# A sparse graph network of two layers: four edits to the attention vectors, the gathers and the column products

## The chip, the cores and the metric

The kernel runs on one core of a Trainium2 chip. The metric is device time in microseconds (us), the median of several runs. An execution recorded by the hardware profiler gives the traces shown here; it has a time of its own, which is stated beside them. TensorE is called PE, VectorE DVE, ScalarE ACT, GpSimd POOL and SyncE SP in the lines of the profile.

## The reference

A graph of 3327 nodes has one dense 0/1 adjacency matrix with ones on its diagonal, about nine ones in a row. Two layers work on 512 features per node, in fp32. Cut to what matters:

```python
def layer0(X, A, W, b, a_self, a_neigh):            # 4 heads of 128
    feats = einsum('nf,hfo->hno', X, W)
    logits = leaky_relu(e_s[:, :, None] + e_n[:, None, :], 0.2) + NEG_INF * (1 - A)
    out = softmax(logits) @ feats + b               # per head
    return relu(out)
x = layernorm(x + layer0(x, adj, ...))

def layer1(x, adj, W_sa, a_sa, W_g, b_g, Wa, ba, Wb, bb):
    gate_a = sigmoid(concat([adj @ x, x]) @ Wa.T + ba)      # gate_b alike
    h = x @ W_sa
    s_left, s_right = h @ a_sa[:512], h @ a_sa[512:]
    e = where(adj, exp(-leaky_relu(s_left + s_right.T, 0.01)), 0)
    x_a = (e / (sum(e) + 1e-5)) @ h
    x_b = adj @ (x @ W_g) + b_g
    return sigmoid(gate_a * x_a + gate_b * x_b)
x = layernorm(x + layer1(x, adj, ...))
```

Since only about nine entries of a row are not zero, the kernel turns each row of the matrix into a list of neighbours and gathers their rows. `s_left` and `s_right` are products of x with two vectors, `W_sa @ a_sa[:512]` and `W_sa @ a_sa[512:]`; these are "W_sa's vectors".

## The kernel before

The 3327 nodes are padded to 3328 and cut into 26 tiles of 128 nodes. The order of instructions on each engine is the order in which the program writes them; a tile framework adds the semaphores.

**Ahead of layer 0.** The node axis is cut into seven chunks of up to 512. For each chunk the kernel computes feature rows (`feature_sums`, L385, `feature_rows`), which go to a table in HBM (`table0`), and reads the chunk's columns of the matrix through 11 buffers with the tag "at" (L228, issued by SP, in order). `make_codes` (L430) packs 16 matrix rows into one number by a matmul with powers of two, `turn_codes` (L455) transposes the codes, `top_codes` takes the largest ones per node on VectorE (L73, L76), and `decode`, `pick`, `name` make neighbour lists of them. W_sa is loaded into two of the same "at" buffers (L244), between the loads of chunks 4 and 5. `scores_vectors` makes the vectors of it: for each of four blocks of 128 rows it transposes the block on PE (L362), copies it on ScalarE (L364), and multiplies it by `a_sa` (L366); the sums go into columns 0 and 3 of `v1`. The tail of the program's first part is `make_codes(4)`, `turn_codes(4)`, `top_codes(4)`, `scores_vectors()`, `make_codes(5)`, `turn_codes(5)`, `climb(0)`. Chunks 4 to 6 hold the second group of tiles; the rest of their lists is made inside layer 0, in its steps 0 to 7 (`lists`).

**Groups and stairs.** Nodes are sorted by degree within two groups of 12 and 14 tiles, so that each tile has a fixed number of neighbours (`CAPS`). The few nodes of very high degree sit in the first tile of each group; their surplus neighbours are spread over the 128 partitions of one extra row, the "stair". `climb` (L661 to L671) makes the list for that extra gather out of the sorted lists by one matmul.

**Layer 0** goes through the tiles in the order `order0`: 11, 10, 0, 1, 2, ... "Place" below is the index in that order. Every row is gathered by an indirect DMA of 128 rows of 520 numbers (L769), issued by POOL; a tile of the second group reads its own two rows by one more (L763), a stair is L778. Before the change the buffers are seven of six rows each, `GB = 7`, `U = 6`; a tile's rows are cut into equal pieces of at most six, one buffer each, and `AHEAD = 3` tiles are asked for in advance:

```python
        n = (c + more + U - 1) // U
        w = (c + more + n - 1) // n
```

Step i of the loop writes, in this order: the gathers of the tile three places on; the publishing of finished tiles (`publish`, with a scatter L147 for the second group); `columns2` of the tile two places back; `attend` of tile i; the relu and residual sum y of the tile before (L1034), its transposes (`columns1`, L940), its statistics; `columns3` of two back (L951); the lists; and the weights of the next tile (`weigh_a` L871 to L890 with the exponential L884, `weigh_b` L895 to L899). `attend` scales each gathered row by its weight, two of three rows on VectorE (L916), the third on ScalarE (L914), and sums them in PSUM by matmuls with the identity (L923). `columns2` copies the transposed tile from PSUM by ScalarE (L944) and multiplies it with the eight columns of `v1` (L947), which gives the scores that layer 1 needs.

**Layer 1** gathers the finished rows from `table1` through the same buffers (L769). Each tile has a weighted sum on VectorE (L1161, with L1163 for sums of two), a plain sum on PE (L1182), two transposes (L1192) and two products with W_sa and W_g (L1201). `weights_a` handles the gathered columns piece by piece: an addition (L1096), a reduction (L1105) and, from the second piece on, one more addition (L1116).

Of the kernel before, what the change touches and what calls it, by code (L numbers as in the profile page):

```python
# [14 lines left out]
P = 128  # L15
# [9 lines left out]
S = 24  # L25
# [6 lines left out]
U = 6  # L32
GB = 7
# [22 lines left out]
def row_bcast(src, n, offset=0):  # L56

    return bass.AP(tensor=src.tensor, offset=src.offset + offset, ap=[[0, P], [1, n]])
# [22 lines left out]
def sparse_pass(  # L81
# [160 lines left out]
    for k in range(0, KT, 2):  # L242
        wsa0 += [p0.tile([P, 2, CH], F32, tag="at", name=f"wsa0_{k}", bufs=AT)]
        nc.sync.dma_start(wsa0[-1], W_sa[k * P : (k + 2) * P, :].rearrange("(k p) o -> p k o", p=P))  # L244
    for i in range(5, len(chunks)):
        load_adj(i, 0, 3)
# [93 lines left out]
    with nc.allow_non_contiguous_dma(reason="four vectors of 512, onto partitions"):  # L340
        for i, w in enumerate((Wa, Wb)):
            for s in range(2):
                src = w[0:1, s * F : (s + 1) * F].rearrange("o (k p) -> p (o k)", p=P)
                nc.gpsimd.dma_start(v1[:, :, 3 * s + 1 + i], src)
        asa = p0.tile([P, KT, 2], F32, name="asa")
        for s in range(2):
            src = a_sa[0:1, s * F : (s + 1) * F].rearrange("o (k p) -> p (o k)", p=P)
            nc.gpsimd.dma_start(asa[:, :, s], src)
# [7 lines left out]
    def scores_vectors():  # L356

        sums = psl.tile([P, CH], F32, tag="pc1", name="asa_sums")[:, : 2 * KT].rearrange("p (k s) -> p k s", s=2)
        for k in range(KT):
            pt = psl.tile([P, CH], F32, tag="pc0", name=f"wsa_t{k}").rearrange("p (o w) -> p o w", o=KT)  # L360
            for o in range(KT):
                nc.tensor.transpose(pt[:, o, :], wsa0[k // 2][:, k % 2, o * P : (o + 1) * P], ident)  # L362
            turned_ = p0.tile([P, KT, P], F32, tag="v", name=f"wsaT{k}", bufs=2)
            nc.scalar.copy(turned_, pt)  # L364
            for o in range(KT):
                nc.tensor.matmul(sums[:, k, :], turned_[:, o, :], asa[:, o, :], start=(o == 0), stop=(o == KT - 1))  # L366
        nc.vector.tensor_copy(v1[:, :, 0], sums[:, :, 1])
        nc.vector.tensor_copy(v1[:, :, 3], sums[:, :, 0])
        nc.vector.tensor_add(v1[:, :, 4:6], v1[:, :, 4:6], v1[:, :, 1:3])
        nc.vector.tensor_add(v1[:, :, 6], v1[:, :, 0], v1[:, :, 3])  # L370
# [349 lines left out]
    make_codes(4)  # L720
    turn_codes(4)
# [4 lines left out]
    climb(0, p0, psl.tile([P, CH], F32, tag="pc0", name="climb0")[:, : B + H])  # L726
# [19 lines left out]
    def gather(table, j):  # L746


        g, i = place(j)
        ahead = 0 if table is table1 else 1 + g  # L750
        c = CAPS[j] + ahead
        more = j in T0
        n = (c + more + U - 1) // U
        w = (c + more + n - 1) // n
        got = []
        for q0 in range(0, c + more, w):
            m = min(w, c - q0)
            buf = gp.tile([P, U, ROW], F32, tag="g", name=f"g_{nc.next_id()}", bufs=GB)
            for q in range(q0, q0 + m):
                s = q - ahead + 1  # L760
                if ahead == 2 and q < 2:
                    if q == 0:
                        nc.gpsimd.indirect_dma_start(  # L763
                            out=buf[:, 0:2, :].rearrange("p t w -> p (t w)"), out_offset=None,
                            in_=own1.rearrange("n t w -> n (t w)"),
                            in_offset=bass.IndirectOffsetOnAxis(ap=srt[g][:, i, S + 1 : S + 2], axis=0),
                        )
                    continue
                nc.gpsimd.indirect_dma_start(  # L769
                    out=buf[:, q - q0, :], out_offset=None, in_=table[:, :],  # L770
                    in_offset=bass.IndirectOffsetOnAxis(ap=srt[g][:, i, s : s + 1], axis=0),
                )
            o = 1 if ahead == 2 and q0 == 0 else 0
            if m > o:
                got.append((q0 + o - ahead + 1, m - o, buf, o))
        if more:
            stair[j] = buf[:, m, :]
            nc.gpsimd.indirect_dma_start(  # L778
                out=stair[j], out_offset=None, in_=table[:, :],
                in_offset=bass.IndirectOffsetOnAxis(ap=ids2[g][:, 0:1], axis=0),  # L780
            )
        return got

    stair = {}
# [78 lines left out]
    got, ws, accs, ws2 = {}, {}, {}, {}  # L863

    def weigh_a(j):
# [20 lines left out]
        for s0, n, buf, o in got[j]:  # L886
            a = max(s0, 1)
            nc.scalar.copy(srt[g][:, i, a : s0 + n], buf[:, o + a - s0 : o + n, F + H])
# [12 lines left out]
    def attend(j, lean):  # L901
# [6 lines left out]
        for s0, n, buf, o in got[j]:  # L908
            for s in range(s0, s0 + n):
                k = 2 if s % 3 == 0 and s + 1 < s0 + n else 1  # L910
                gv = buf[:, o + s - s0 : o + s - s0 + k, 0:F].rearrange("p t (h o) -> p t h o", h=H)
                if s % 3 == 2:
                    for h in range(H):
                        nc.scalar.activation(gv[:, 0, h, :], gv[:, 0, h, :], AF.Copy, scale=w[:, s, h : h + 1])  # L914
                elif s % 3 == 0 or s == s0:
                    nc.vector.tensor_tensor(  # L916
                        gv, gv, w[:, s : s + k, :].rearrange("p t (h o) -> p t h o", o=1).to_broadcast([P, k, H, FO]),
                        ALU.mult,
                    )
                row = buf[:, o + s - s0, 0:F]  # L920
                if lean and s == 0:
                    nc.vector.tensor_add(row, row, bias0)
                nc.tensor.matmul(  # L923
                    acc, ident, row, start=(lean and s == 0), stop=(s == CAPS[j] and j not in T0)
                )
        if j in T0:
# [14 lines left out]

    def columns2(j):
        xt1 = m0.tile([P, KT, P], F32, tag="xt1", name=f"xt1_{j}")
        nc.scalar.copy(xt1, turned[j])  # L944
# [21 lines left out]
    AHEAD = 3  # L966
    for j in order0[:4]:
        own_x(j)
    for i in range(AHEAD):
        got[order0[i]] = gather(table0, order0[i])  # L970
# [41 lines left out]
    for i in range(NT + 3):  # L1012
# [7 lines left out]
        if i + AHEAD < NT:  # L1020
            j = order0[i + AHEAD]
            got[j] = gather(table0, j)
# [3 lines left out]
        if 2 <= i < NT + 2:  # L1026
            columns2(order0[i - 2])
        if i < NT:
            attend(order0[i], i >= 3)
        if 0 < i <= NT:  # L1030
# [3 lines left out]
            nc.vector.scalar_tensor_tensor(y, accs[j], 0.0, xj, ALU.max, ALU.add)  # L1034
            columns1(j)
# [170 lines left out]
    for i in range(3):  # L1206
        got[at_(i)] = gather(table1, at_(i))
# [5 lines left out]
    for i in range(NT + 3):  # L1213
        j, j1, jp, jpp = at_(i), at_(i + 1), at_(i - 1), at_(i - 2)
        if at_(i + 3) is not None:
            got[at_(i + 3)] = gather(table1, at_(i + 3))
# [494 lines left out]
```

## Time and profile before

| | us |
|---|---|
| median of 3 runs | 998.16 |
| lowest and highest | 991.17, 1000.08 |
| the profiled execution | 1102.09 |
| its span, first to last instruction | 1100.0 |

The profiled execution's granted PE clock is 0.856 of full speed in the mean. Over its span PE is busy 845.0 us (77%), VectorE 723.8 (66%), POOL 611.7 (56%), ScalarE 281.9 (26%).

| stage of the profiled execution | from, us | to, us |
|---|---|---|
| feature rows, codes, lists of the first group | 0 | 152 |
| chunk 5's codes, W_sa's vectors, first gathers | 152 | 205 |
| layer 0, places 0 to 8 with the lists of chunks 4 to 6 | 205 | 410 |
| layer 0, places 9 to 25 | 410 | 655 |
| layer 1, start | 655 | 720 |
| layer 1 | 720 | 1100 |

How to read it: a group's line has its line in the kernel, engine and operation, what it writes and reads, shapes and count; then its busy time and the mean of one in ns; then the idle time of its engine just before it, with what ended most of that. "Issue" is waiting for nothing that the profile shows; "remote" is a wait that ended by a semaphore for which no record of the profile stands. A fp32 matmul has two records, and a matmul's end is modelled, so its mean can be longer than the distance to the next one. Times are from the start of the span.

### The profile page before, as it was taken

Reading aid. Unit: us, or ns where it says so; the run is one execution under the profiler, and the core shown is the slowest. Engines: PE = TensorE matmul, PEld = TensorE weight load, DVE = VectorE, ACT = ScalarE, POOL = GpSimd, SP = SyncE. Lnnn points to the kernel's source line nnn. Section 1 sums busy time; section 2 is a strip of 40 time slices with the busy share of each in tenths; the row PEclk is TensorE's granted clock in tenths of the full one; section 3 lists DMA queues with packets and bytes.
Section 4 is the critical chain, followed back from the end, with each engine's and each line's share of the span. In section 5 each row is a group of like instructions: output and inputs, shape, how many; then the busy total and the mean of one; then the engine's idle time right before and its main releaser. Section 6 shows DMA issues by size and latency. Waiting matters only on the chain.

```text
span 1100.0 us, 10256 instructions
## 1 busy us (share of the span) xinstructions
PE 845.0 (77%) x2596; PEld 450.0 (41%) x2596; DVE 723.8 (66%) x2179; ACT 281.9 (26%) x824; POOL 611.7 (56%) x663
## 2 busy tenths in 40 slices
PE   6999761755785877668897685399797978997994
PEld 5777641322433333334443341144343434443442
DVE  3367740563895676556764574379797997997893
ACT  1122110220412132323434231032233213232322
POOL 6011646555474227467777627737777776777502
PEclk9999965668787879699888886699899998998998
DMA  9899888857966227487667616735666664666401
GB/s 320 351 372 409 313 325 305 258 156 230 317 171 180 68 83 218 141 299 205 187 195 207 197 50 185 203 108 155 196 172 187 183 193 147 188 189 176 123 10 60
DMA packets 72850, 220.89 MB, mean 201 GB/s; under 512 B 11472, under 2 KB 16544, under 8 KB 72016
## 3 DMA queue, kind: packets, MB, share of 16 engines
q0 software_dynamic: 44592, 146.73, 45.1%
q1 hardware_dynamic: 23200, 62.32, 15.2%
q10 hardware_dynamic: 4992, 11.12, 2.7%
q8 instruction: 23, 0.38, 0.1%
q14 instruction: 43, 0.35, 0.1%
HBM read 199.26 MB, written 28.32 MB: 207 GB/s over the span
## 4 chain that ended last, share of the span: by engine, by line
PE 36%; DVE 20%; issue 15%; POOL 9%; DMA 8%; another core or an unknown queue 8%; ACT 3%; DVEq 0%; ACTq 0%; POOLq 0%; SPq 0%
PE acc L923 15%; POOL g L769 8%; DVE sw L1161 7%; PE pf L385 7%; PE po L1201 5%; DMA g<-table,srt 4%; PE acc L1182 4%; DMA at<-in_adjB 3%; DVE g L1163 2%; PE pcol L947 2%; DVE g L916 1%; DMA xc<-in_xB 1%; PE pc L430 1%; ACT g L914 1%
## 5 line engine op out<-in xcount | busy, mean ns | idle before, releaser
L769 POOL DMA_INDIRECT g<-table,srt x464 | 489.0, 1054 | 265.8 <-issue 130.3
L923 PE MATMUL acc<-g,ident 128*128 128x512 f32 x504 | 265.9, 690 | 9.0 <-issue 5.6
L1161 DVE SCALAR_TENSOR_TENSOR sw<-g,e,sw 128x512 f32<-128x512 f32 x226 | 169.4, 750 | 12.8 <-issue 4.5
L923 PEld LDWEIGHTS acc<-g,ident 128*128 128x128 f32 x504 | 110.6, 225 | 147.9 <-issue 132.0
L1182 PE MATMUL acc<-g,ident 128*128 128x512 f32 x262 | 123.4, 606 | 13.1 <-DMA g<-table,srt 9.7
L1201 PE MATMUL po<-wsa,sT 128*128 128x512 f32 x208 | 99.8, 624 | 24.9 <-issue 16.2
L385 PE MATMUL pf<-w,xc 128*128 128x260 f32 (+1 forms) x416 | 102.7, 410 | 15.6 <-DMA xc<-in_xB 10.6
L916 DVE TENSOR_TENSOR g<-g,w 128x1024 f32<-128x1024 f32 (+1 forms) x102 | 105.1, 1073 | 1.1 <-DVE w L897 0.5
L385 PEld LDWEIGHTS pf<-w,xc 128*128 128x128 f32 x416 | 84.7, 206 | 31.4 <-issue 10.5
L947 PE MATMUL pcol<-v,xt 128*128 128x8 f32 x208 | 37.0, 305 | 78.5 <-ACT xt L944 39.1
L1201 PE MATMUL po<-wg,sT 128*128 128x512 f32 x208 | 93.7, 593 | 0.0
L914 ACT ACTIVATE g<-g,w 128x128 f32<-128x128 f32 x304 | 92.1, 393 | 0.9 <-issue 0.9
L1182 PEld LDWEIGHTS acc<-g,ident 128*128 128x128 f32 x262 | 50.2, 194 | 80.3 <-issue 52.0
L1201 PEld LDWEIGHTS po<-wsa,sT 128*128 128x128 f32 x208 | 41.2, 201 | 80.6 <-issue 69.3
L947 PEld LDWEIGHTS pcol<-v,xt 128*128 128x128 f32 x208 | 34.7, 252 | 85.1 <-ACT xt L944 43.4
L1163 DVE TENSOR_TENSOR g<-g 128x512 f32<-128x512 f32 x95 | 65.7, 692 | 3.3
L147 POOL DMA_INDIRECT out<-za,srt x26 | 29.0, 1117 | 58.6 <-ACT za L1246 52.5
L1194 ACT COPY sT<-pt 128x512 f32<-128x512 f32 x52 | 29.0, 588 | 120.6 <-remote 51.1
L1201 PEld LDWEIGHTS po<-wg,sT 128*128 128x128 f32 x208 | 39.4, 190 | 48.8 <-issue 48.3
L884 ACT ACTIVATE w<-w 128x40 f32<-128x40 f32 (+10 forms) x26 | 6.2, 238 | 192.9 <-DVE w L883 102.2
L73 DVE MAX8 ent<-pv 128x8 f32<-128x224 f32 x26 | 10.0, 386 | 51.9 <-PE pv L455 51.9
L401 ACT COPY row<-pf 128x512 f32<-128x512 f32 x26 | 15.3, 587 | 104.2 <-PE pf L385 66.6
(279 smaller groups left out, 948.8 us busy)
## 6 DMA issues: line engine op xcount, KB each, us to landing
at<-in_adjB SPq DMA_DIRECT2D x78, 512.0 KB
g<-table,srt POOLq DMA_INDIRECT x464
table<-row ACTq DMA_DIRECT2D x26, 260.0 KB
own<-in_xo SPq DMA_DIRECT2D x1, 3640.0 KB
own<-table SPq DMA_DIRECT2D x1, 3640.0 KB
at<-in_adjL SPq DMA_DIRECT2D x13, 256.0 KB
table<-x1a SPq DMA_DIRECT2D x12, 260.0 KB
xc<-in_xB ACTq DMA_DIRECT2D x3, 1024.0 KB
```

What stands on the lines that cost most here:

```text
L147: put = nc.gpsimd.indirect_dma_start(out=dst, out_offset=bass.IndirectOffsetOnAxis(ap=rows, axis=0), in_=src, in_offset=None, bounds_check ...
L385: nc.tensor.matmul(pf[:, hh, :w], xc[:, k, o : o + P], w0[:, k, hh, :w], start=(k == 0), stop=(k == KT - 1))
L769: nc.gpsimd.indirect_dma_start(out=buf[:, q - q0, :], out_offset=None, in_=table[:, :], in_offset=bass.IndirectOffsetOnAxis(ap=srt[g][:, i ...
L914: nc.scalar.activation(gv[:, 0, h, :], gv[:, 0, h, :], AF.Copy, scale=w[:, s, h : h + 1])
L916: nc.vector.tensor_tensor(gv, gv, w[:, s : s + k, :].rearrange("p t (h o) -> p t h o", o=1).to_broadcast([P, k, H, FO]), ALU.mult,)
L923: nc.tensor.matmul(acc, ident, row, start=(lean and s == 0), stop=(s == CAPS[j] and j not in T0))
L947: nc.tensor.matmul(pcol, xt1[:, k, :], v1[:, k, :], start=(k == 0), stop=(k == KT - 1))
L1161: nc.vector.scalar_tensor_tensor(sw, g[:, i, 0:F], e[:, s : s + 1], sw, ALU.mult, ALU.add)
L1163: nc.vector.tensor_add(g[:, i, 0:F], g[:, i - 1, 0:F], g[:, i, 0:F])
L1182: nc.tensor.matmul(plain[j], to, row, start=(not sums_of_two and i == 0), stop=(sums_of_two and i == len(rows) - 1),)
L1194: nc.scalar.copy(sT, pt)
L1201: nc.tensor.matmul(proj[j], sT[:, k, :], wt[:, k, :], start=(half + k == 0), stop=(half + k == KT))
```

## The change

- `scores_vectors` makes W_sa's vectors on VectorE: for each half of `a_sa` and each of four blocks of W_sa one product with a sum (`tensor_tensor_reduce`) straight into a column of `v1`. `a_sa` comes as two rows spread over all partitions, into a third "at" buffer, behind W_sa in SP's queue. The products are written into the pool `pj`, which is given back before the ring's memory is taken.
- `climb(0)` moves ahead of `turn_codes(4)`.
- The buffers of the gathers become one tile of 42 rows, `ring`. `plan` lays out all tiles of a layer in it one after another; a tile is cut only where the ring ends. `gather` issues, in order, whatever fits into 42 rows past the last tile that is given back by `free`. In layer 0 `gather` and `free` now stand behind y of the tile before, in layer 1 at the head of the step.
- `columns2` is split: ScalarE's copy (`columns2a`) stays ahead of `attend`, the eight matmuls are issued inside it, behind the rows 0 to 2 of the sum.

```diff
+    asa_rows = p0.tile([P, 2, CH], F32, tag="at", name="asa_rows", bufs=AT)
+    for s in range(2):
+        nc.sync.dma_start(asa_rows[:, s, :], row_bcast(a_sa, F, s * F))
...
     def scores_vectors():
-        sums = psl.tile([P, CH], F32, tag="pc1", name="asa_sums")[:, : 2 * KT].rearrange("p (k s) -> p k s", s=2)
-        for k in range(KT):
-            pt = psl.tile([P, CH], F32, tag="pc0", name=f"wsa_t{k}").rearrange("p (o w) -> p o w", o=KT)
-            for o in range(KT):
-                nc.tensor.transpose(pt[:, o, :], wsa0[k // 2][:, k % 2, o * P : (o + 1) * P], ident)
-            turned_ = p0.tile([P, KT, P], F32, tag="v", name=f"wsaT{k}", bufs=2)
-            nc.scalar.copy(turned_, pt)
-            for o in range(KT):
-                nc.tensor.matmul(sums[:, k, :], turned_[:, o, :], asa[:, o, :], start=(o == 0), stop=(o == KT - 1))
-        nc.vector.tensor_copy(v1[:, :, 0], sums[:, :, 1])
-        nc.vector.tensor_copy(v1[:, :, 3], sums[:, :, 0])
+        for s in range(2):
+            for k in range(KT):
+                prod = pj.tile([P, ROW], F32, tag="row", name=f"sprod{s}_{k}", bufs=4)[:, :F]
+                nc.vector.tensor_tensor_reduce(
+                    prod, wsa0[k // 2][:, k % 2, :], asa_rows[:, s, :], 1.0, 0.0, ALU.mult, ALU.add,
+                    v1[:, k, 3 - 3 * s : 4 - 3 * s],
+                )
...
     make_codes(4)
+    climb(0, p0, psl.tile([P, CH], F32, tag="pc0", name="climb0")[:, : B + H])
     turn_codes(4)
     top_codes(4)
     scores_vectors()
     make_codes(5)
     turn_codes(5)
-    climb(0, p0, psl.tile([P, CH], F32, tag="pc0", name="climb0")[:, : B + H])
...
+    ring = gp.tile([P, RING, ROW], F32, name="ring")
...
+        while s <= CAPS[j]:
+            n = 2 if own_x_too and s == 0 else 1
+            if planned[0] % RING + n > RING:
+                planned[0] += 1
+            p = planned[0] % RING
+            m = min(CAPS[j] + 1 - s + n - 1, RING - p)
+            buf = ring[:, p : p + m, :]
+            got[j].append((s, m - (n - 1), buf, n - 1))
...
+    def gather():
+        while waiting and waiting[0][0] - freed[0] <= RING:
+            indirect(*waiting.pop(0)[1:])
+
+    def free(j):
+        freed[0] = ends_at[j]
...
-        if 2 <= i < NT + 2:
-            columns2(order0[i - 2])
+        third = order0[i - 2] if 2 <= i < NT + 2 else None
+        if third is not None:
+            columns2a(third)
         if i < NT:
-            attend(order0[i], i >= 3)
+            attend(order0[i], i >= 3, lambda: third is None or columns2(third))
+        elif third is not None:
+            columns2(third)
...
             nc.vector.scalar_tensor_tensor(y, accs[j], 0.0, xj, ALU.max, ALU.add)
+            free(j)
+            gather()
             columns1(j)
```

In layer 1 the loop calls `free(jp)` for the tile before and `gather()` at the head of its step, in place of asking for the tile three places on.

## The prediction, made before the changed kernel ran

> **What bounds the kernel now.** I read first the busy time by stage (columns: stretch, length, busy time and instructions of PE, PE's weight loads, VectorE, ScalarE, POOL; then the granted PE clock, the share of the DMA engines and GB/s).
>
> ```profile
> 152.00:205.00 53.00, 21.23 (x100) 14.77 (x98) 11.69 (x46) 5.97 (x13) 29.16 (x31) 0.50 0.92 331
> 205.00:410.00 205.00, 144.27 (x371) 69.89 (x372) 137.47 (x459) 49.44 (x169) 99.95 (x99) 0.78 0.58 177
> 410.00:655.00 245.00, 191.36 (x535) 97.84 (x533) 148.37 (x426) 85.22 (x267) 156.28 (x144) 0.86 0.61 188
> 720.00:1100.00 380.00, 332.75 (x897) 156.67 (x895) 316.87 (x766) 105.20 (x241) 229.96 (x211) 0.95 0.51 148
> ```
>
> Layer 1 (from 720) is full: PE is busy 88%, VectorE 83%. Layer 0 (205 to 655) is not: no engine is busy over 78%. So layer 0 waits for something, and the waits (us in total, times, longest) say for what. POOL between 340 and 480, then VectorE between 410 and 625:
>
> ```profile
> POOL g L769 <- PE acc L923: 40.6, 5, 18.5
> POOL g L763 <- issue: 9.8, 4, 8.8
> POOL g L769 <- ACT x1a L955: 9.4, 1, 9.4
> POOL g L769 <- DVE x1b L1034: 5.9, 1, 5.9
> ```
>
> ```profile
> DVE w L871 <- DMA g<-table,srt: 30.5, 7, 6.4
> ```
>
> First POOL, which issues the gathers, stands idle for a free buffer (8.8+18.5+12.6+9.4+8.8+5.9 = 64 us from 346 to 474); later VectorE stands idle for the gathers. The timeline of POOL against the exponentials (L884) gives the lead of a tile's last gather: 52 us at the tenth tile of the order, 12 at the 13th, and 4.0 to 7.6 from the 16th to the 24th, where the landing alone takes some 3. From 482 to 622 POOL issues without a break of over 2.5 us: there the gather stream is the bound, and it is late because it could not run ahead before.
>
> The stretch ahead of layer 0, from the timeline (start, length, instruction, idle time before it and what ended it):
>
> ```profile
> 152.24 0.95 POOL L769 DMA_INDIRECT g<-table,srt  x1 [7.09 <-DMA wsa<-in_W_sa]
> ...
> 167.19 0.59 ACT L364 COPY wsaT<-wsa_t 128x512 f32<-128x512 f32 x1 [8.32 <-remote]
> ...
> 186.07 0.95 POOL L769 DMA_INDIRECT g<-table,srt  x1 [0.30 <-issue]
> 189.61 0.59 ACT L364 COPY wsaT<-wsa_t 128x512 f32<-128x512 f32 x1 [21.83 <-remote]
> ...
> 192.04 2.32 PE L430 MATMUL pc<-at,pow 128*32 128x512 bf16 x18
> ...
> 201.78 0.95 POOL L778 DMA_INDIRECT g<-table,ids  x1 [14.76 <-DVE es L671]
> ```
>
> Chunk 5's codes (L430) stand behind W_sa's turn on PE, climb behind those, and the stair gather L778 behind climb: POOL loses 14.8 us. The odd part is "remote": the last transposes are recorded at 170.2, their semaphore comes at 189.5. No record explains these 19 us (and 5.5 before 167.2). The profiled execution took 1102.09 us, 104 more than the median of 998.16, so such waits may belong to the profiling. I count them at half.
>
> The rows used below (busy, mean ns | idle before):
>
> ```profile
> L769 POOL DMA_INDIRECT g<-table,srt x464 | 489.0, 1054 | 265.8 <-issue 130.3 <-PE acc L923 41.2 <-PE acc L1182 25.5
> L1161 DVE SCALAR_TENSOR_TENSOR sw<-g,e,sw 128x512 f32<-128x512 f32 x226 | 169.4, 750 | 12.8 <-issue 4.5 <-ACT sw L1145 4.1
> L947 PE MATMUL pcol<-v,xt 128*128 128x8 f32 x208 | 37.0, 305 | 78.5 <-ACT xt L944 39.1 <-issue 36.2 <-ACT w L884 3.2
> L1105 DVE TENSOR_REDUCE gate<-g 128x2 f32<-128x10 f32 (+3 forms) x49 | 6.0, 160 | 0.2 <-issue 0.2
> L871 DVE TENSOR_TENSOR w<-g,srt 128x20 f32<-128x20 f32 (+3 forms) x55 | 9.2, 178 | 32.6 <-DMA g<-table,srt 30.9 <-issue 0.6 <-DMA at<-in_adjL 0.5
> ```
>
> **What the skill says.** (1) The Trainium skill, "DMA: Bandwidth & Descriptors", SWDGE vs HWDGE vs iDMA: software on GpSimd writes the descriptors of a DMA issued there. The trace agrees: each gather holds POOL 0.95 us at least, plus 0.30 to the next, whether it has one wait or three. (2) The same skill, "SBUF — State Buffer", SBUF: two separate sides: VectorE in a two-port mode locks GpSimd out of their shared port, so descriptors come late. It fits, without proof, that a gather takes 0.95 where VectorE is idle (152 to 187) and 1.05 in the mean. (3) The same skill, "TensorE: Matmul & The Clock Gate", Part 1: about 3.4 us of idling halve PE's clock. The trace agrees: the granted clock is 0.50 from 152 to 205 and 0.95 in layer 1. Gaps cost twice.
>
> **The change part by part.**
>
> *Vectors on VectorE.* PE loses 16 transposes (L362) and 32 records of small products (L366, 7.5 us), ScalarE four copies, POOL two small loads. VectorE gets eight products of 128x512. No such row is there: L309's 128x128 form takes 289 ns plus an 84 ns read of the sum, so the bounds are 0.5 us (fixed cost shared) and 1.24 (four times 289, plus 84). I take L1161's 0.75 plus 0.08 less overlap, 0.8: 6.4 us for eight. They stand behind chunk 4's top codes, which end at 161.8 (a little later, as climb's four small operations, 0.6 us, now go ahead), so they end near 168.5. SP issues two more loads of 256 KB ahead of chunk 5's: 1.5 us at 331 GB/s, beside waiting anyway; they take a third of the 11 buffers "at" until 168.5, so five of chunk 5's 13 loads come after that: 2.6 MB, 8 to 13 us, then 2 us for codes and turn. The first sum can start near 185 instead of 205.2.
>
> *A new wait.* The products are written into the pool pj (tag row), and the ring lies where pj lay. In the built program the first gather waits for the eighth product. Everything on POOL is behind it: the stream starts at 168.5, not 152.24, 16.3 us late. Against that the stair gather no longer waits 14.8: it comes at 168.5 + 28 x 1.25 = 203.5 against 201.8. After it 13 more gathers precede the eight loads of own rows, all done by 231, as before (230.7). Tile 3's exponentials are at 276.5, minus 20: still 25 us of lead, so the early tiles are not held up; VectorE's list work paces them. Net for the start: -20 if the remote waits are real, about +2 if not. I take -10.
>
> *Climb earlier.* Two matmuls (0.5 us) and a wait on PE for two copies from the sorted lists, which are on chip at 140.4, before PE gets there at 152.1. Nothing waits; if the lists were late, chunk 4's turn would stand behind them.
>
> *The ring.* Before, seven buffers of six rows, filled with 3.5 to 6 rows, and at most three tiles ahead; after, 42 rows, freed row by row (each gather waits for the matmul that read its row). At 410 nine tiles, 94 rows, are consumed: the stream can stand at row 136, and stood at about 121. At 478, 141 are consumed: 183 against about 159. One row costs 1.36 us in that stretch (92 rows from 457.3 to 601.7, less 19.5 us of waits, over 92, publishing scatters included). So 15 to 24 rows are 20 to 33 us; I take -27. The stream has the time: 183 rows and 8 loads at 1.33 us from 168.5 end at 422. Cover for the rest: PE needs for the 16 tiles from 410 about 160 rows x 0.86 + 16 x 2 us = 170, VectorE 148, both under the 215 left.
>
> *Columns inside the next sum.* They fill PE's wait for ScalarE's copy, in all 78.5 us ahead of L947. Where PE is the bound a tile gains about 1 us; where the sum waits for its weights, the columns' 1.06 to 1.88 us were free and now lengthen the sum. With the gathers as bound most of it is slack. VectorE's L951 comes three rows (2.6 us) later, behind its other work. Bounds -12 and +5, taken -3.
>
> *Fewer pieces.* Layer 1 has 18 pieces fewer, each three small VectorE operations (0.23+0.16+0.16): -9.9 us of VectorE work; layer 0 26 times 0.18 = 4.6 us, and ScalarE 27 casts. In layer 1 PE is as full, so of 9.9 I count -4 (0 to -9). Layer 1's gathers lead by 8.6 us or more once it is under way; the ring gives nothing there.
>
> Sum: -10 - 27 - 3 - 4 = -44 against 1102.1, i.e. 1058, 0.96 of it. On the median: 958 us. A measurement of this kernel tells about 1% from no change (its three runs lie 0.9% apart).
>
> **The rivals.** (A) *All of it*, 20%: remote waits real (-20), ring -35, columns -8 as PE's clock stays up, pieces -7: -70, 1032 of 1102, 935 us. For it: the clock 0.86 in layer 0. Against: the 104 us that only the profiled execution has. (B) *The work takes over*, 15%: with gathers early, PE at half clock and VectorE's chain from y to the next weights pace the late tiles; only -6 is left: 993 us. For it: after its gathers a tile still takes 9.5 to 10 us. Against: the 30.5 us in which VectorE waits for nothing else. (C) *The late first gather*, 10%, slower: if outside the profile climb is never late and the stream never idles for buffers, it is one chain from first row to last, and its 16.3 us land on the end; less 4 for the pieces, +12, 1009 us. It decides once POOL's 64 us of waiting for buffers fall under 16. Against: layer 0's lists pace the early tiles at some 23 us each (205 us for nine), ten rows of the stream take 13.
>
> My forecast has 55% (945 to 980 alone). The range 930 to 995 takes in A and most of B. Faster 0.77, same 0.14, slower 0.09.
>
> **What would show it.** First gather near 168, no wait of 14 us at the stair; POOL's waits for PE from 340 to 480 smaller, the lead at the 16th to 24th tile over 10 us; L871's wait on gathers under 10 us; layer 0's length down by about 35 us; layer 1 shorter by under 10. Wrong if leads are long and layer 0 as long as before (B), or if leads are 4 us from early on (C).

## The result and the profile after the change

| | before | after |
|---|---|---|
| median of 20 runs each, us | 997.40 | 990.15 |
| lowest, highest | 990.12, 1001.79 | 986.00, 994.59 |
| ratio of the runs, with its 95% interval | | 0.9932 (0.9912 to 0.9952) |
| the profiled execution shown here, its span | | 990.03, 988.3 |

The change gains 0.7%, 7 us, where 40 were forecast. The time lies inside the range given, beside rival B's 993, but far above the forecast.

On some chips the kernel before takes about 997 us and on others about 1110, and its first profile came from the slower kind, the profile after from the faster one, so these two can't be set against each other. The kernel before was therefore traced again on a chip of the faster kind (the run e8_before below, span 997.9 us), and the comparisons here are with that trace.

The stages of the kernel after (columns as in the prediction: stretch, length, busy time and instructions of PE, PE's weight loads, VectorE, ScalarE, POOL; PE clock, DMA share, GB/s):

```profile
152.00:205.00 53.00, 30.46 (x82) 12.63 (x79) 29.50 (x119) 10.53 (x35) 35.66 (x36) 0.66 0.93 320
205.00:410.00 205.00, 156.07 (x443) 75.37 (x443) 152.29 (x468) 60.97 (x194) 136.76 (x128) 0.85 0.71 223
410.00:590.00 180.00, 142.22 (x420) 70.66 (x419) 113.74 (x305) 64.89 (x189) 124.79 (x112) 0.89 0.64 196
640.00:985.00 345.00, 321.18 (x872) 148.88 (x870) 300.41 (x688) 98.19 (x231) 237.37 (x220) 0.98 0.61 171
```

The same stretches of the kernel before on the faster kind of chip:

```profile
152.00:205.00 53.00, 33.48 (x111) 17.29 (x110) 23.09 (x106) 8.26 (x25) 40.18 (x42) 0.67 0.99 362
205.00:410.00 205.00, 158.55 (x440) 79.06 (x440) 150.44 (x488) 62.22 (x209) 118.11 (x114) 0.83 0.64 202
410.00:590.00 180.00, 152.31 (x426) 75.73 (x426) 117.39 (x315) 67.99 (x212) 130.85 (x118) 0.88 0.69 209
640.00:985.00 345.00, 325.13 (x885) 150.79 (x883) 307.48 (x738) 99.06 (x230) 240.13 (x220) 0.99 0.61 171
```

Up to 410 POOL does more after the change (136.8 us busy against 118.1): the ring does let the gathers run ahead. But from 410 on layer 0 is as before: PE busy 79% after, 85% before, no engine full. Layer 1 (the last row) has 50 fewer VectorE instructions and 7 us less of them.

The rows of the kernel after that answer to those of the prediction (busy, mean ns | idle before, and what ended it):

```profile
L746 POOL DMA_INDIRECT ring<-table,srt x464 | 500.8, 1079 | 175.5 <-issue 77.1 <-DMA ring<-table,srt 27.7 <-DVE x1b L1050 18.2
L1179 DVE SCALAR_TENSOR_TENSOR sw<-ring,e,sw 128x512 f32<-128x512 f32 x226 | 169.3, 749 | 10.7 <-ACT sw L1163 4.0 <-PE pt L1210 2.7
L963 PE MATMUL pcol<-v,xt 128*128 128x8 f32 x208 | 26.2, 253 | 1.5 <-ACT xt L957 1.5
L1123 DVE TENSOR_REDUCE gate<-ring 128x2 f32<-128x12 f32 (+11 forms) x31 | 4.9, 170 | 0.0
L878 DVE TENSOR_TENSOR w<-ring,srt 128x36 f32<-128x36 f32 (+12 forms) x29 | 5.6, 195 | 60.4 <-DMA ring<-table,srt 56.3 <-DMA ring<-table,ids 2.1 <-issue 1.0
```

The last row is the one that the forecast lived on. VectorE was to wait under 10 us for the gathers of layer 0; it waits 56.3 us, against 40.7 in e8_before; 13.2 of the 56.3 lie ahead of the first tile, the rest from the 13th tile on. L963 shows the columns' wait gone (1.5 us), and L1123 the pieces: 31 in place of 49.

Two of POOL's waits in the timeline of the kernel after (start, length, instruction, idle time before it and what ended it):

```profile
158.42 0.94 POOL L746 DMA_INDIRECT ring<-table,srt  x1 [11.12 <-PE pc L424]
...
410.20 0.94 POOL L746 DMA_INDIRECT ring<-table,srt  x1 [16.06 <-DVE x1b L1050]
...
421.63 0.94 POOL L746 DMA_INDIRECT ring<-table,srt  x1 [2.15 <-DVE x1b L1050]
```

The first is the new wait ahead of the first gather, some 11 us. The eighth product ends at 157.56, 0.86 us ahead of the gather, and the distance is 0.85 or 0.86 us in all ten traces in which the products are written into `pj`, whatever the profile names there; so the product ended the wait, and not the matmul. The second is the ring, full: the next gather overwrites the own row of the 13th tile, and L1050, which makes that tile's y, still has to read it. POOL stands 16 us, then 2 more for the 14th.

### The profile page after: what moved, and what is told of

Same layout as the page of the kernel before. It is cut to its first block, busy times and chain, and to the rows that moved or that the text cites. A ratio compares the mean times of both kernels' runs of the same rounds, so it can differ in the third digit from the quotient of the medians.

```text
span 988.3 us, 10334 instructions
## 1 busy us (share of the span) xinstructions
PE 809.8 (82%) x2548; PEld 420.3 (43%) x2548; DVE 720.4 (73%) x2104; ACT 275.0 (28%) x793; POOL 620.2 (63%) x661
## 5 line engine op out<-in xcount | busy, mean ns | idle before, releaser
L746 POOL DMA_INDIRECT ring<-table,srt x464 | 500.8, 1079 | 175.5 <-issue 77.1
L932 PE MATMUL acc<-ring,ident 128*128 128x512 f32 x504 | 263.7, 675 | 73.9 <-DVE ring L931 67.6
L932 PEld LDWEIGHTS acc<-ring,ident 128*128 128x128 f32 x504 | 102.7, 214 | 197.9 <-issue 103.5
L1179 DVE SCALAR_TENSOR_TENSOR sw<-ring,e,sw 128x512 f32<-128x512 f32 x226 | 169.3, 749 | 10.7 <-ACT sw L1163 4.0
L1200 PE MATMUL acc<-ring,ident 128*128 128x512 f32 x262 | 126.8, 613 | 20.2 <-DVE ring L1181 10.3
L925 DVE TENSOR_TENSOR ring<-ring,w 128x1024 f32<-128x1024 f32 (+1 forms) x93 | 104.5, 1162 | 0.6
L923 ACT ACTIVATE ring<-ring,w 128x128 f32<-128x128 f32 x304 | 91.6, 388 | 1.3 <-DVE w L906 1.0
L1200 PEld LDWEIGHTS acc<-ring,ident 128*128 128x128 f32 x262 | 49.3, 193 | 90.1 <-issue 44.9
L1181 DVE TENSOR_TENSOR ring<-ring 128x512 f32<-128x512 f32 x95 | 65.7, 692 | 3.3
L1251 ACT ACTIVATE za<-za 128x512 f32<-128x512 f32 x26 | 16.4, 631 | 156.5 <-DVE za L1249 156.5
L878 DVE TENSOR_TENSOR w<-ring,srt 128x36 f32<-128x36 f32 (+12 forms) x29 | 5.6, 195 | 60.4 <-DMA ring<-table,srt 56.3
L424 PE MATMUL pc<-at,pow 128*32 128x512 bf16 (+1 forms) x182 | 23.7, 415 | 30.0 <-DMA at<-in_adjB 22.7
```

The source lines that it names most:

```text
L424: nc.tensor.matmul(pc[32 * c : 32 * c + 32, : nt * P], pow2[:, s, :], loaded[i, m], start=(s == 0), stop=(m + 1 not in ms or s == 3),)
L746: nc.gpsimd.indirect_dma_start(out=out_, out_offset=None, in_=table, in_offset=bass.IndirectOffsetOnAxis(ap=ap, axis=0))
L925: nc.vector.tensor_tensor(gv, gv, w[:, s : s + k, :].rearrange("p t (h o) -> p t h o", o=1).to_broadcast([P, k, H, FO]), ALU.mult,)
L932: nc.tensor.matmul(acc, ident, row, start=(lean and s == 0), stop=(s == CAPS[j] and j not in T0))
L1179: nc.vector.scalar_tensor_tensor(sw, g[:, i, 0:F], e[:, s : s + 1], sw, ALU.mult, ALU.add)
L1181: nc.vector.tensor_add(g[:, i, 0:F], g[:, i - 1, 0:F], g[:, i, 0:F])
```

## The experiments

The runs e0 to e7 and e12 to e16 met chips of the slower kind and settle little by themselves; e8 to e11 and e17, on one chip of the faster kind, carry the argument.

### The kernel before again, and three edits alone (slower kind of chip)

e0_before is the kernel before, unchanged.

> The kernel before once more, for a second trace. Both theories: the unexplained waits of the first trace (19 us ahead of chunk 5's codes, and the others marked remote) are gone, and the profiled execution takes about 1000 us instead of 1102. Then the layer boundaries can be compared with those of the changed kernel: layer 0's last y at about 590 us, layer 1's length about 395 us, first sum near 180 us. If the waits are there again (over 1080 us), they belong to the kernel, and the change removed them.

Measured 1106.23 us; the median of 59 runs of the kernel before beside it was 1115.21. The trace is that of the first profile: L364 waits 17.7 us for "remote", and the stair gather 15.1 us. The recorded execution of e8 further below takes 999.92 us on another chip, so these waits and the 104 us that I had put down to the recording belong to the chip.

e1_vectors_climb takes the first two edits alone:

```diff
+    asa_rows = p0.tile([P, 2, CH], F32, tag="at", name="asa_rows", bufs=AT)
...
+                nc.vector.tensor_tensor_reduce(
...
     make_codes(4)
+    climb(0, p0, psl.tile([P, CH], F32, tag="pc0", name="climb0")[:, : B + H])
     turn_codes(4)
```

> Only the vectors on VectorE and the early climb, buffers and columns as before. Theory 1 (small parts, all the same way): -2 us, the stair gather comes earlier, nothing else moves; 993 to 998 us. Theory 2 (parts of opposite sign): the late first gather costs, since the gather stream is one chain; +4 to +10 us, 1001 to 1007 us.

e2_ring takes the ring alone:

```diff
+RING = 42
...
+    ring = gp.tile([P, RING, ROW], F32, name="ring")
...
+            free(j)
+            gather()
             columns1(j)
```

> Only the ring, vectors, climb and columns as before. Theory 1: the ring gives no lead where the stream is the bound; it brings only the fewer pieces of layer 1, -2 to -5 us, 992 to 995 us. Theory 2: it brings what was forecast, -15 to -27 us, 970 to 982 us, and the other parts eat it.

e3_columns takes the columns alone:

```diff
+                if s == 2:
+                    between()
```

> Only the columns' products inside the next sum. Theory 1: they fill a wait of PE that is slack where gathers are the bound; 0 to -4 us, 993 to 997 us. Theory 2: they lengthen the sums that wait for their weights; +2 to +6 us, 999 to 1003 us.

Measured ratios to the kernel before: 0.9974 (0.993 to 1.0017), 1.004 (0.9958 to 1.0122), 0.995 (0.9897 to 1.0003). None is told from no change, and the ring's 27 us are not there. But e2's trace showed where to look: the lead, from the end of a tile's last gather to its exponential, is 34 to 76 us up to the 13th tile and 7.9 at the 16th.

### Products elsewhere, columns undone, gathers thinned (slower kind of chip)

e4_before is the kernel before once more; e5 writes the products where the first gather doesn't wait for them; e6 is the change with the columns ahead of the sum again; e7 leaves out every third gather of the last eleven tiles of layer 0, whose sums are done on whatever lies in the ring.

```diff
-                prod = pj.tile([P, ROW], F32, tag="row", name=f"sprod{s}_{k}", bufs=4)[:, :F]
+                prod = p0.tile([P, 2, CH], F32, tag="v", name=f"sprod{s}_{k}", bufs=2)[:, 0, :F]
```

```diff
-                waiting.append((planned[0], buf[:, k, :], table[:, :], srt[g][:, i, s : s + 1]))
+                if not (table is table0 and j in order0[15:] and s % 3 == 2):
+                    waiting.append((planned[0], buf[:, k, :], table[:, :], srt[g][:, i, s : s + 1]))
```

> The kernel before a third time. On the first chip of these experiments it took 1106 to 1115 us, where the 20 runs above gave 997, and its trace has the unexplained waits again; so they go with the chip. Theory: on a chip that runs it in about 997 us the trace shows no wait of 19 us ahead of chunk 5's codes, the first sum at 178 to 185 us, the y of place 12 at 410 to 415 us, layer 0's last y at 583 to 590 us, and layer 1 as long as in the changed kernel or up to 5 us longer. On a slow chip: the same trace as before, 1100 us.

> The changed kernel, but the products of W_sa's vectors are written into buffers that do not lie under the ring, so that the first gather does not wait for them. Theory (the late first gather holds up the start, and layer 0's early tiles shift with it): first gather 5 to 6 us earlier, every place of layer 0 3 to 5 us earlier, 3 to 5 us faster than the changed kernel, 0.988 to 0.990 of before. Rival (the start is set by chunk 5's codes on TensorE, or the time is taken up later): under 1 us against the changed kernel.

> The changed kernel with the column products ahead of the sum, as before. Theory (they gain about 1 us per tile where TensorE is the bound, in places 9 to 16 alone): 3 to 6 us slower than the changed kernel, 0.997 to 0.999 of before. Rival (slack): within 1 us of the changed kernel, 0.993.

> The changed kernel without every third gather (rows 2, 5, 8, 11 of the list) of places 15 to 25 of layer 0: those rows keep what lay in the ring, the sums and all later work are done on them as before, so a part of the input of these sums is left out. POOL has about 33 gathers fewer. Theory (the stream of gathers is the bound there): VectorE's waits for gathers in that stretch nearly vanish, and layer 0's last y comes 20 to 28 us earlier, until TensorE is the bound. Rival (TensorE and VectorE set the pace): under 5 us earlier.

Measured: e4 1110.23 us (median of 25 runs of the kernel before beside it: 1108.4); e5 1.0105 (1.0064 to 1.0145); e6 1.0262 (1.0194 to 1.0329); e7 1093.97 us in one run. On this kind of chip versions of the change are slower than the kernel before, which I hadn't expected; the change itself was not run there. e5's trace settles what the first gather waits for: with the products elsewhere it comes at 151.6, 14 us before the eighth product ends. What e7 shows lies in a stretch of its trace: from y of the 16th tile to the last y it takes 111 us, while the change takes 139 (442.7 to 581.5 in the profile shown above). PE and VectorE can do these ten tiles in 111 us or less; what holds them is the stream of gathers. That spoke against rival B.

### Before, after and the two halves on one chip (faster kind)

e8_before is the kernel before, e9_after the change, both unchanged. e10_all_but_ring has vectors, climb and columns, with the old buffers; e11_ring_alone is the kernel of e2.

> The kernel before once more, for a trace from the chip on which the next three kernels run. If the chip is of the kind that takes 997 us: no unexplained waits over 6 us on PE, VectorE or ScalarE (the trace after the change has none), W_sa's vectors done near 172, first sum near 185, stair gather waiting under 5 us; the lead of the last gather 15 to 60 us up to the tenth tile and 4 to 8 us from the 16th on, as in the first trace. If it is of the kind that takes 1110 us: the trace of the first profile again, span near 1105, some fifteen such waits.

> The kernel after the change, beside the kernel before on the same chip. Theory S (the stream of gathers from the 13th tile to the last is as long as before; what was gained are small parts elsewhere): ratio 0.993, as measured, on a chip that takes 997 us. On a chip that takes 1110 us the unexplained waits are as many in both, and the ratio is 0.99 to 1.00. Theory R (the ring gains some 27 us where the unexplained waits don't cover it): 0.97 to 0.98 on the slower kind of chip.

> Vectors, climb and columns as changed, the gathers through seven buffers of six rows as before. Theory S (the ring is worth nothing at the end of layer 0): ratio 0.995, all of the change's gain but the fewer pieces of layer 1 (2 to 4 us). Theory R (the gain is the ring's): 1.000, within 0.003.

> The ring alone, W_sa's vectors, climb and columns as before. Theory S: 0.997 to 1.000; the ring has long leads up to the 12th tile, stands full while the 13th tile waits for its sum, and from the 16th on the lead is 4 to 8 us as before. Theory R: 0.993 to 0.995, and the exponentials of the last ten tiles come 5 us or more earlier after y of the 13th than in the kernel before.

Measured ratios: e9 0.9932 (0.9911 to 0.9952), as before; e10 1.0024 (1.0005 to 1.0042); e11 0.9912 (0.9882 to 0.9942). The whole gain is the ring's; the other three edits together give nothing, or cost 0.2%. Theory S falls, but theory R's place for the gain is wrong too. From the five traces of this chip (times in us from the start of the span, rows by the end of their gather; the last column is of the run further below):

| | before e8 | all but ring e10 | ring alone e11 | after e9 | after, late scatters e17 |
|---|---|---|---|---|---|
| first gather | 150.9 | 158.7 | 148.3 | 161.5 | 158.4 |
| first exponential | 180.7 | 172.1 | 184.5 | 175.0 | 171.8 |
| y of the 9th tile | 367.8 | 366.8 | 370.7 | 367.6 | 361.9 |
| y of the 13th tile | 415.2 | 415.1 | 416.5 | 413.7 | 408.0 |
| 161st row issued | 429.5 | 429.7 | 423.6 | 420.8 | 415.1 |
| 254th, last row issued | 565.8 | 565.9 | 567.7 | 566.5 | 549.2 |
| last y of layer 0 | 585.4 | 585.2 | 586.0 | 585.8 | 566.7 |
| layer 1, first gather to end | 400.9 | 400.4 | 394.2 | 395.4 | 392.8 |

In the first four, layer 0 ends within 0.8 us of the same time. Part of that is chance, since two executions of one kernel differ by 4 us there (581.5 in the first trace of the change, 585.8 in e9); but from y of the 13th tile to the last y it takes 170.3, 170.1, 169.5 and 172.1 us, and 172.3 in the first trace of the change, so the late tiles gained nothing. In these traces the gain, 5.5 to 6.7 us, is all in layer 1. There the two traces differ in VectorE's small operations on pieces. The kernel before, on this chip (group lines; L1105 reduces a piece, L1116 adds it):

```profile
L1105 DVE TENSOR_REDUCE gate<-g 128x2 f32<-128x10 f32 (+3 forms) x49 | 6.0, 159 | 0.2 <-issue 0.2
...
L1116 DVE TENSOR_TENSOR gate<-gate 128x2 f32<-128x2 f32 x25 | 4.0, 161 | 0.9
```

and the change (L1123, L1134 are the same two lines):

```profile
L1123 DVE TENSOR_REDUCE gate<-ring 128x2 f32<-128x12 f32 (+11 forms) x31 | 4.9, 170 | 0.0
...
L1134 DVE TENSOR_TENSOR gate<-gate 128x2 f32<-128x2 f32 x7 | 1.1, 160 | 0.2
```

From layer 1's first gather to the end VectorE has 54 instructions fewer in e9 (820 to 766), which is three for each of 18 pieces, and 6.9 us less to do (339.9 to 333.0), about the length by which layer 1 is shorter. A longer lead of the gathers is no rival there: VectorE waits for gathered rows as long in both (17.6 us and 18.3), and so does PE (9.6 and 9.7). That these operations are the cause is still argued from the traces; the run that was to show it (e14) met the slower kind of chip.

Then the columns. PE's waits in the kernel before, from the list of waits (us in total, times, longest):

```profile
PE pcol L947 <- ACT xt L944: 47.5, 24, 6.6
...
PE acc L923 <- DVE g L922: 7.2, 10, 0.9
```

and in all but the ring (L917 is L922 there, VectorE's addition of the bias to a tile's own row):

```profile
PE acc L918 <- DVE g L917: 68.1, 19, 8.5
```

The wait for ScalarE's copy is gone; PE gets to the sum earlier and waits there for VectorE instead. The wait has moved. And VectorE, whose copy of the products into the row (L953, L951 before) was hardly held up in e8 (twice 0.6 us), now waits for them in e10:

```profile
DVE x1a L953 <- PE pcol L949: 9.2, 5, 2.7
...
DVE x1b L953 <- PE pcol L949: 8.5, 6, 2.6
```

### Where the ring's lead goes: the scatters

In the table the change has its 161st row out 8.7 us before the old kernel, and its last row 0.7 us after it. From the one to the other the stream takes 145.7 us, 136.4 before. What stands between the gathers differs. In the kernel before, POOL's timeline at the end of the stream has the second four scatters behind the last gather:

```profile
563.62 0.94 POOL L769 DMA_INDIRECT g<-table,srt  x1 [0.30 <-issue]
564.87 0.95 POOL L769 DMA_INDIRECT g<-table,srt  x1 [0.30 <-DMA g<-own,srt]
566.12 1.02 POOL L147 DMA_INDIRECT table<-x1b,srt  x1 [0.30 <-issue]
```

In the change (e9) the same four stand eight rows ahead of its end:

```profile
549.74 1.43 POOL L746 DMA_INDIRECT ring<-table,srt  x1 [0.30 <-issue]
551.48 1.03 POOL L146 DMA_INDIRECT table<-x1b,srt  x1 [0.30 <-issue]
552.81 1.00 POOL L146 DMA_INDIRECT table<-x1b,srt  x1 [0.30 <-issue]
554.12 0.99 POOL L146 DMA_INDIRECT table<-x1b,srt  x1 [0.30 <-issue]
555.41 0.99 POOL L146 DMA_INDIRECT table<-x1b,srt  x1 [0.30 <-issue]
556.70 0.99 POOL L746 DMA_INDIRECT ring<-table,srt  x1 [0.30 <-issue]
...
565.52 0.95 POOL L746 DMA_INDIRECT ring<-table,srt  x1 [0.30 <-issue]
```

Four at 1.3 us are 5.2 of the 9.3 us. The rest is the wait for y of the 14th tile (1.9 more than a plain distance of 0.30) and gathers that take 2.2 us longer in all. The order is the program's: at step 22 the old kernel had asked for three tiles ahead, that is for all rows, before it published; the change has asked for 42 rows past the last tile given back, and its `gather()` stands behind `publish` in the step.

So the next kernel, e12_after_late_scatters, holds all scatters of layer 0 back until the last gather is issued:

```diff
+    held = []
+
+    def let_go():
+        for j in held:
+            scatter("table1", table1[:, :], own(j), row1(j), N - 1)
+        held.clear()
...
-            scatter("table1", table1[:, :], own(j), row1(j), N - 1)
+            held.append(j)
...
+        if not waiting:
+            let_go()
...
             gather()
+            if not waiting:
+                let_go()
```

e13_before_late_scatters does this to the kernel before (there with `if i + AHEAD >= NT - 1` behind `publish`), e15_ring_late_scatters to the ring alone. e14_after_old_pieces cuts layer 1's rows as before:

```diff
+        many = CAPS[j] + (j in T0)
+        width = -(-many // -(-many // 6)) if table is table1 else RING
...
-            m = min(CAPS[j] + 1 - s + n - 1, RING - p)
+            m = min(CAPS[j] + 1 - s + n - 1, RING - p, width)
...
```

> The change, with all scatters of layer 0 held back until its last gather is issued; after the change eight of the fourteen stand ahead of it. Theory Q (the lead that the ring gives is spent on scatters that moved ahead of the last gathers): eight scatters at 1.3 us leave the stream, the last gather is issued 8 to 10 us earlier, near 556, the last sum comes near 576 instead of 586, the time is near 983, ratio to before 0.982 to 0.987. Theory W (PE and VectorE are the bound of the last ten tiles): the last gather is earlier, leads grow, the last sum stays within 3 us of 586, ratio 0.991 to 0.994.

> The kernel before with the scatters held back in the same way; only four of the fourteen stood ahead of its last gather. Theory Q: four times 1.3 us, 5 us earlier at the last gather and at the last sum, ratio 0.995 (0.993 to 0.997). Theory W: 0.999 to 1.001.

> The change, with layer 1's rows handled in pieces of at most six, as before (they still lie in the ring, so a few pieces are cut once more at its end). If layer 1's gain is the VectorE operations on pieces: layer 1 takes 400 to 402 us again and the ratio is 0.999 to 1.003. If it is the order and the lead of the gathers: layer 1 stays at 395 us and the ratio at 0.993.

> The ring alone with late scatters; vectors, climb and columns as before. If these three are worth nothing at layer 0's end even with a faster stream: the same as the change with late scatters, within 0.2%. If they were hidden only by the stream: 3 to 8 us slower than that.

They met the slower kind of chip (the kernel before at 1120.48 us): e12 1.0359 (1.0248 to 1.047), e13 1.0007 (0.9941 to 1.0073), e14 1150.31 us, e15 1.0136 (0.9969 to 1.0304). Waits that no record explains lie across the last ten tiles there, 14 and 17 us on VectorE in e12, 20 and 19 in e14, so neither theory can be read from them. e14's layer 1 takes 450.0 us there, with the old pieces, and those of e12 and e15, with the new ones, 456.8 and 449.7. e16 is e12's kernel again:

> The change with all scatters of layer 0 held back until its last gather is issued, once more. On a chip that takes 997 us for the kernel before: theory Q (the ring's lead is spent on scatters that moved ahead of the last gathers): last gather near 556, last sum near 576, ratio 0.982 to 0.987. Theory W (PE and VectorE are the bound of the last ten tiles): last sum within 3 us of 586, ratio 0.991 to 0.994. On a chip of the slower kind: 1.02 to 1.04 again, nothing settled.

The slower kind once more: 1.0199 (1.0115 to 1.0283). e17, again the same kernel, met the chip of e8 to e11:

> The change with all scatters of layer 0 held back until its last gather is issued, a third time. On a chip that takes 997 us for the kernel before: theory Q (the ring's lead is spent on scatters that moved ahead of the last gathers): last gather near 556, last sum near 576, ratio 0.982 to 0.987. Theory W (PE and VectorE are the bound of the last ten tiles): last sum within 3 us of 586, ratio 0.991 to 0.994. On a chip of the slower kind: 1.02 to 1.04 again, nothing settled.

Measured 975.92 us against 996.65 for the kernel before, 0.9801 (0.9764 to 0.9839): theory Q, a little beyond its 0.982 to 0.987, and a kernel faster than both. POOL's timeline at the end of its stream:

```profile
547.01 0.95 POOL L746 DMA_INDIRECT ring<-table,srt  x1 [0.30 <-PE acc L932]
548.26 0.95 POOL L746 DMA_INDIRECT ring<-table,srt  x1 [0.30 <-issue]
549.51 1.45 POOL L146 DMA_INDIRECT table<-x1b,srt  x1 [0.30 <-DMA ring<-table,srt]
...
565.00 0.98 POOL L146 DMA_INDIRECT table<-x1b,srt  x1 [0.30 <-issue]
572.13 0.98 POOL L146 DMA_INDIRECT table<-x1b,srt  x1 [6.15 <-DVE x1b L982]
```

Eleven scatters now fill the time in which POOL has nothing else to do. The 93 rows take 134.1 us, 11.5 less than in e9, of which eight scatters at 1.3 us are 10.4. The last sums, y of the 13th tile and of the last, in the timeline of e9:

```profile
413.70 0.68 DVE L1050 SCALAR_TENSOR_TENSOR x1b<-acc,ring 128x512 f32<-128x512 f32 x1
...
585.80 0.69 DVE L1050 SCALAR_TENSOR_TENSOR x1b<-acc,ring 128x512 f32<-128x512 f32 x1 [1.61 <-PE acc L932]
```

and of e17:

```profile
407.96 0.68 DVE L1059 SCALAR_TENSOR_TENSOR x1b<-acc,ring 128x512 f32<-128x512 f32 x1
...
566.69 0.69 DVE L1059 SCALAR_TENSOR_TENSOR x1b<-acc,ring 128x512 f32<-128x512 f32 x1 [1.04 <-PE acc L932]
```

From one to the other 172.1 and 158.7 us: 13.4 less. The 5.7 us by which e17 is ahead at its 13th tile are not the edit's: e9's first scatter of finished tiles comes only at 490.5, and two executions of the change itself differ at that y by 4.5. VectorE's wait for gathered rows from the 13th tile on, in e8, e9 and e17 (us in total, times, longest):

```profile
DVE w L871 <- DMA g<-table,srt: 38.5, 9, 6.3
...
DVE w L878 <- DMA ring<-table,srt: 43.0, 8, 9.7
...
DVE w L878 <- DMA ring<-table,srt: 30.4, 8, 5.0
```

The ring alone didn't shorten these waits; the late scatters did. The leads of the 18th to the 24th tile are still 4 to 5 us in e17, so the stream of gathers is the bound there yet. Whether the ring is needed for this gain isn't settled: the old kernel with late scatters ran only where nothing could be told, and it has only four scatters to move.

## Why the prediction was wrong, step by step

**What bounds the kernel.** Right in its core: the stream of gathers bounds layer 0's second half, as e7 and e17 show. Wrong in its base: the "remote" waits, counted at half as belonging to the recording, go with the chip. On the faster kind none of PE, VectorE and ScalarE has an unexplained wait over 6 us after 150 us, before or after the change. One reading beside it was wrong too: VectorE is not idle from 152 to 187 in the first profile, it picks maxima until 161.8, and the gathers issued beside that take 0.95 us as well. Sorted by what VectorE does at the same time, e8's gathers take 0.95 us in the mean beside nothing (71, the longest 0.99), 0.95 beside instructions of under 512 columns alone (112, the longest 1.18), and 1.15 where one of 512 columns or more overlaps them (299, up to 2.00). This fits the prediction's second point; what property of these instructions does it isn't shown.

**Vectors and the new wait: -10 taken, 0 at the end of layer 0 (with climb and columns, in e10).** The eight products take 0.69 us each, 0.61 apart, 5.0 us and not 6.4. The first gather comes 8 to 11 us late (16 forecast), since POOL does wait for the eighth. The early tiles weren't free of it: VectorE waits 13 us for the first tile's gathers, and the leads of the first five are 5.5 to 14 us, not 25. The first exponential comes 8.6 us earlier in e10 than in e8, the fourth 4.6, y of the ninth tile 1.0 and y of the 13th 0.1. In between VectorE waits 9.0 us for gathered rows in e10, all at the third and fourth tile, and 0.5 in e8, so a part goes back to the late stream. Another 3.1 us go between y of the seventh tile and of the ninth, where the gathers lead by 37 and 48 us in e10, so not to them: VectorE waits there 2.3 us for the columns' products and 5.5 for climb, where e8 has none and 4.5. VectorE's own work from the first exponential to that y is nearly the same (139.1 us and 137.6). And from the 13th tile on the old kernel and e10 wait for the same buffers (leads 5.5 and 5.4 us at the 14th). I had carried a gain at the start through all 26 tiles unchanged. The stair's 14.8 us don't exist on this chip: the stair gather follows the one before it after 0.30 us.

**The ring: -27 taken, 8.7 us reached, none kept. This step failed, twice.** First in its size. The position at the ninth tile was right: row 136 forecast, 134 in e9, about 121 in e8. But at y of the 14th tile I took 183 as the position, and that is what the ring allows only once this tile's rows are given back; at that moment 13 tiles are, and the stream stands at 163, the old one at 159. POOL stands idle for 16 us until y of the 13th tile, issues seven rows, and finds the ring full again 2 us ahead of the next y. The 42 rows hold few tiles there: the 14th, 15th and 16th alone fill 39. Second, "so many rows are so many us" assumed the stream behind them unchanged. I gave 1.36 us per row "publishing scatters included" (8.8 of the 19.5 us of waits taken off lie ahead of that stretch; without them it is 1.45), while the change moves four scatters from behind the last gather to ahead of it. The Trainium skill, "DMA: Bandwidth & Descriptors", SWDGE vs HWDGE vs iDMA, says that software on GpSimd writes the descriptors of what is issued there; a scatter costs POOL 0.99 + 0.30 us in the trace, as much as a row. I named POOL's queue for the first gather, and didn't follow it for the step's other half.

**Columns: -3 taken, about 0.** PE's wait for the copy went (47.5 us to 1.5) and came back as a wait for VectorE (7.2 to 68.1). That VectorE's copy of the columns comes "behind its other work" was wrong: it waits 17.7 us for the products in e10, 1.2 in e8. Apart from the other edits they ran only on the slower kind of chip (e3).

**Fewer pieces: -4 taken, -5.5 to -6.7 for layer 1 as a whole.** Right in kind and within its bounds of 0 to -9; VectorE has 6.9 us less to do, 9.9 forecast. In the traces layer 1 holds all of the change's gain, though that the pieces are its cause is only argued.

**The rivals.** B's time is right and its reason wrong: leads stay at 4 us from the 18th tile to the 24th, so PE and VectorE didn't take over. C had short leads from early on for its sign, and they are about 50 us at the tenth to 12th tile; its price is wrong as well, as the late first gather was made up by the ninth tile. That the time lies inside the range is luck: the range was stretched towards B, and B's cause didn't come about. The sign "L871's wait under 10 us" was the one that told at once.

## What to carry to other kernels

A longer look-ahead pays only as far as the queue that uses it goes on: ask at each step how full the buffer is when the next row may be overwritten, and list everything else in that queue, which moves against the stream when the look-ahead changes. Transfers that nobody waits for yet belong behind the last one that somebody waits for. And settle which kind of chip a trace came from before its waits are given a meaning.

## What the runs showed of the hardware

The same kernel takes 997 us on one chip (two measurements, medians 996.65 and 998.12, clock 0.893 in the trace) and 1108 to 1120 us on four others (0.850 and 0.857 where it was traced). The slower ones show waits of 6 to 45 us whose end no record explains, often at the same place of the program. In e16, PE in the timeline:

```profile
189.31 1.10 PE L916 MATMUL acc<-bias,ident 128*128 128x512 f32 x2
227.60 9.10 PE L932 MATMUL acc<-ring,ident 128*128 128x512 f32 x14 [37.19 <-issue]
```

The same instruction waits 44.5 us in e12. On the faster chip there is no such wait. Three versions of the change are slower on such chips than the kernel before (ratios of 1.01 to 1.04), one of which, with late scatters, is 2% faster on the faster chip. What these waits are stays open.
